# Transposing the float16 pairs of p, queries and keys: from DMA to TensorE, in an attention kernel with a gated feed-forward part

## The chip, the core and the metric

The kernel runs on one core of one Trainium2 chip. A core has TensorE (PE in the profile: matmuls out of the on-chip memory SBUF into the eight banks of PSUM; PEld is its weight load), VectorE (DVE), ScalarE (ACT), GpSimd (POOL) and SyncE (SP), which here only issues DMAs. The metric is the device time of one execution in microseconds. A time "before" and a time "after" are medians of several runs; the profile is of one execution, with its own time beside it.

## The reference

With x of 1024 rows and 512 columns, the result is x + s * g, where xn is x normalised by row:

```python
xn = _layernorm(x, axis=-1)
s = _L0_attn_ref(xn, Wq, Wk, Wv, Wo, q_norm_w, k_norm_w)
g = _silu(_L0_ffn_ref(xn, gate_w, gate_z, gate_s, up_w, up_z, up_s, down_w, down_z, down_s))
x = x + s * g
...
# attention: 32 heads in 8 groups of 4 that share keys and values, head size 128
q = _rmsnorm(q, q_norm_w)
k = _rmsnorm(k, k_norm_w)
scores = jnp.einsum('bkgqd,bksd->bkgqs', qg, k) / math.sqrt(HD)
rel = pos[None, :] - pos[:, None]
bias = jnp.where(rel > 0, NEG_INF, slopes[:, :, None, None] * rel)
attn = jax.nn.softmax(scores + bias[None], axis=-1)
out = jnp.einsum('bkgqs,bksd->bkgqd', attn, v)
return out.transpose(0, 2, 1, 3).reshape(b, s, H * HD) @ Wo.T
# feed-forward: integer weights of three matrices, dequantised by groups of 128 rows
gate = jax.nn.silu(jnp.dot(x, gate_proj))
return jnp.dot(gate * jnp.dot(x, up_proj), down_proj)
```

The attention is causal, with a bias that is linear in the distance (another slope for each head).

## The kernel before

The data is float32. Most matmuls run on pairs of float16 numbers: a value is split in a high half and what is left of it, and a product of two pairs takes three matmuls, hi*hi, hi*lo and lo*hi, into one sum. This is the helper `mm3`, whose three matmuls are lines 114, 115 and 116; so these three lines stand for many different products in the profile, told apart by the names of their tiles.

The order of the work on every engine is written out by hand, and every engine takes its instructions strictly in that order. There are three stages.

**Feed-forward (0 to about 235 us).** Layer norm, float32 transpositions of xn by TensorE (`xt_ps`, line 361, after 40 warming ones, `warm`, line 383, and a spread of the zeros, `z_ps`, line 188), gate and up products (`gu_ps`), the down product (`dn_ps`). Its result goes to `gd` in DRAM. The stage has its own PSUM pool.

**Projections (about 235 to 490 us).** Twelve projections run one after the other, each in eight tiles of 128 rows: for each pair of groups one for keys and values (`ps_kv`), then two for queries (`ps_q`, four heads each). A tile is 12 matmuls of 512 columns (`tile`, line 597). ACT copies it out (`f_q`, `f_kv`, line 607) and takes the squares (`jk`, line 609); POOL multiplies by the inverse norms; DVE makes the pair `a16` (`halves`, line 667). Scores need queries and keys with the head dimension on the partitions, so each pair has to be transposed: `transposed` (line 687) issues a transposing DMA on SP into `tr`, and `store` writes that to DRAM (`qd`, `kd`). The pairs of the last projection but one are stored as they are and transposed when they are loaded (`load_queries`, line 846); those of the last one stay in SBUF and are transposed from there (`last_queries`, line 858). With the last two projections the first eight steps of attention are interleaved (`early_tile`, line 1076).

**Attention (to the end).** A unit is one head and one block qb of 256 queries; its two steps, qt 0 and 1, are its tiles of 128 queries. The order of units goes by groups, in a group by blocks (qb 2, 3, 0, 1; the first group 3, 2, 1, 0 and the last 2, 3, 1, 0), in a block by its four heads. There are 128 units and 256 steps. Because of the causal mask, step (qb, qt) has 2*qb+qt+1 key tiles of 128. What `step` (line 1084) issues at n:

- `scores(n)` (line 903): 3 matmuls for each 512 keys into `s`, two buffers of two PSUM banks each;
- ACT: `heads_hi` (L991), when the unit whose values ended in the step before was complete;
- `biased(n-1)` on DVE (L923): scores plus bias, with the row's least; `exponentials(n-1)` on ACT (L929); `split_hi(n-3)` on ACT (L948) and `split_lo(n-4)` on DVE (L957), which make the pair of p;
- DVE: `heads_lo` (L996), then `accumulate` (L1030), which adds a finished `op` to y;
- `values(n-9)` (line 969): half of the unit's products `av` of p and values, into a bank `o`, with up to two `out_proj` in between (`op`, bank `m`, one accumulation over four heads).

`av` needs p with the keys on the partitions. So at its end `split_lo` issues a transposing DMA on SP (line 965) from `p` into `pT`, one for a step, or one for a whole unit with qb 0 (line 960), whose missing blocks are zeroed. Four `pT` buffers exist. PSUM in the last two stages: two buffers `s` of two banks each, two banks `o` and two banks `m`. SP's queue also issues every load and store.

Of the kernel before, what the change touches and what calls it, by code (L numbers as in the profile page):

```python
# [10 lines left out]
F32 = mybir.dt.float32  # L11
# [65 lines left out]
def attention_gated_by_ffn_kernel(ctx, tc, x, gu_w, gu_z, gu_s, dn_w, dn_z, dn_s, wq, wkv, wo, qnw, knw, out):  # L77
# [8 lines left out]
        return psum[0].tile([P, 2, 512], F32, tag="s", name=name)  # L86

    def ps1(tag, name):
        return psum[0].tile([P, 512], F32, tag=tag, name=name)

    def rsqrt_seed(v, y):

# [25 lines left out]

    ident = const.tile([P, P], F32, name="ident")
    make_identity(nc, ident)  # L120
    ones_bf = const.tile([P, P], BF16, name="ones_bf")
    ve.memset(ones_bf, 1.0)
    rv = const.tile([P, HKV], F32, name="rv")
# [362 lines left out]
    def finish_step():  # L486

        for f in finishing.pop(clock[0], ()):
            f()
        clock[0] += 1  # L490

    def defer(steps, f):
        finishing.setdefault(clock[0] + steps, []).append(f)
# [4 lines left out]
    class Projection:  # L498
# [98 lines left out]
        def tile(self, t):  # L597
            n, half, r = self.n, t // HT, t % HT
            if r == 0:
                self.f[half] = fq.tile([P, HT, n, HD], F32, tag="f", name=f"f_{self.name}_{half}", bufs=4)  # L600
                self.ss[half] = fq.tile([P, HT, n], F32, tag="ss", name=f"ss_{self.name}_{half}", bufs=3)
                self.jk = wp.tile([P, NH, HD], BF16, tag="jk", name=f"jk_{self.name}_{half}")
            ps = ps1("o" if t % 2 else "m", f"ps_{self.name}_{t}")
            rows = slice(t * P, (t + 1) * P)
            for j in range(KT):
                mm3(ps, (xth[:, j, rows], xtl[:, j, rows]), (self.wh[:, j, :], self.wl[:, j, :]), j == 0, j == KT - 1)
            se.copy(self.f[half][:, r], ps[:, : n * HD].rearrange("p (g d) -> p g d", g=n))
            for i in range(n):
                se.activation(
                    self.jk[:, i],  # L610
                    ps[:, i * HD : (i + 1) * HD],
                    AF.Square,
                    scale=STEEPER[i] / Q_SCALE if self.kind == "q" else 1.0,
                    accum_out=self.ss[half][:, r, i : i + 1],
                )
            if self.kind == "kv":
                if t == 0:
                    self.v16 = vp16.tile([P, 2, NT, 2, HD], F16, tag="v16", name=f"v16_{self.i}")
                v16 = self.v16[:, :, t]
                vp = ps[:, 256:512].rearrange("p (g d) -> p g d", g=2)  # L620
                se.copy(v16[:, :, 0, :], vp)
                defer(1, lambda: ve.tensor_tensor(v16[:, :, 1, :], vp, v16[:, :, 0, :], ALU.subtract))
                if t == NT - 1:
                    defer(3, self.store_values)
# [42 lines left out]
        def halves(self, t):  # L667
            f = self.f[t // HT][:, t % HT]
            n = self.n
            if self.kind == "q":  # L670
                a16 = fq.tile([P, 2, n, HD], F16, tag="a16", name=f"q16_{self.i}_{t}", bufs=5)
                hi, lo = a16[:, 0], a16[:, 1]
            else:
                a16 = fq.tile([P, 2, 2, HD], F16, tag="a16", name=f"k16_{self.i}_{t}", bufs=5)
                hi, lo = a16[:, :, 0, :], a16[:, :, 1, :]
                ve.tensor_tensor(f, f, wn.unsqueeze(1).to_broadcast([P, 2, HD]), ALU.mult)
            ve.tensor_copy(hi, f)
            ve.tensor_tensor(lo, f, hi, ALU.subtract)
            if self.k == len(projections) - 1:
                last_pairs[t] = a16  # L680
            elif self.k == len(projections) - 2:

                defer(1, lambda: sp.dma_start(qd[self.i][t], a16.rearrange("p a g d -> p (a g d)")))
            else:
                defer(1, lambda: self.transposed(t, a16))

        def transposed(self, t, a16):
            tr = fq.tile([P, 2 * self.n, P], F16, tag="tr", name=f"tr_{self.name}_{t}", bufs=5)
            sp.dma_start_transpose(tr, a16.rearrange("p a g d -> p (a g d)"))
            defer(2, lambda: self.store(t, tr))  # L690

        def store(self, t, tr):
            if self.kind == "q":
# [151 lines left out]

    def load_queries(g, qb):
        qT[g, qb] = ap1.tile([P, NQT, 2, NH, P], F16, tag="qT", name=f"qT{g}_{qb}", bufs=2)
        if g == HKV - 2:
            for i in range(NQT):
                sp.dma_start_transpose(qT[g, qb][:, i].rearrange("p a g q -> p (a g) q"), qd[g][qb * NQT + i])  # L850
            return
        sp.dma_start(
            qT[g, qb].rearrange("p t a g q -> p t (a g q)"), qd[g][qb * NQT : (qb + 1) * NQT].rearrange("t p c -> p t c")
        )
# [3 lines left out]
    def last_queries(t):  # L858
        g, qb = HKV - 1, t // NQT
        if (g, qb) not in qT:  # L860
            qT[g, qb] = ap1.tile([P, NQT, 2, NH, P], F16, tag="qT", name=f"qT{g}_{qb}", bufs=2)
        sp.dma_start_transpose(
            qT[g, qb][:, t % NQT].rearrange("p a g q -> p (a g) q"), last_pairs.pop(t).rearrange("p a g d -> p (a g d)")
        )

    def wo_squares_sums():
        ve.tensor_tensor(rvs, rv, rv, ALU.mult)
# [82 lines left out]
    def split_lo(u, qt):  # L950
        p, h16 = pf.pop((u, qt)), p16.pop((u, qt))
        nk = p.shape[1]
        if qt == 0:
            pool, tag = (wide, "wide") if u % 4 < 2 else (pt_pool, "pT")
            pT[u] = pool.tile([P, NT, 2, QB], F16, tag=tag, name=f"pT{u}", bufs=2)
        hi, lo, scale = h16[:, :, 0, :], h16[:, :, 1, :], rows16[u][3][:, qt : qt + 1]
        ve.scalar_tensor_tensor(lo, p, scale, hi, ALU.mult, ALU.subtract)  # L957
        if u in p16:
            if qt == NQT - 1:
                sp.dma_start_transpose(  # L960
                    pT[u][:, :NQT].rearrange("p t a (i q) -> p (t a i) q", i=NQT),
                    p16.pop(u).rearrange("p t a i k -> p (t a i k)"),
                )
            return
        sp.dma_start_transpose(
            pT[u][:, :nk, :, qt * P : qt * P + P].rearrange("p t a q -> p (t a) q"), h16.rearrange("p t a k -> p (t a k)")
        )

    def values(u, part, between):
# [105 lines left out]

    def early_tile(c):

        if c % 2 == 0:
            scores(*at(c // 2))
        for stage, lag in ((biased, 1), (exponentials, 2), (split_hi, 5), (split_lo, 6)):  # L1080
            if (c - lag) >= 0 and (c - lag) % 2 == 0:
                advance(stage, (c - lag) // 2)

    def step(n):
        nonlocal last_ps
        if n < nn:
            u, qt = order[n]
            g, qb, hh = units[u]
# [21 lines left out]
        if n < nn + AV_LAG + 1:  # L1110
            for due in acc_at.get(n, ()):
                accumulate(*due)
        finish_step()

        def project():
            for due in op_at.get(n, ()):
                out_proj(*due)

        if at(n - AV_LAG):
            values(*at(n - AV_LAG), project)  # L1120
        else:
            project()
# [102 lines left out]
```

## Time and profile before

| | |
|---|---|
| median of 3 runs | 1050.61 us (1048.09 to 1052.13) |
| the profiled execution | 1050.74 us, its span 1049.0 us |
| granted TensorE clock, mean | 0.991 |
| busy in the span: PE, DVE, ACT, POOL | 999.9, 877.8, 799.9, 424.3 us |
| DMA packets | 455007, of which 401474 under 512 B; 203.34 MB |
| transposing DMAs | 224 for p, 48 and 32 for queries and keys, 16 more for queries |
| median time to landing, p | 4.1 us |

A row of instructions gives the engine, the line, the tile written, the tiles read, the shape, the count, the busy time and the mean duration; then the idle time of the engine just before, with what ended it. Matmuls are pipelined: the duration of one is longer than the distance to the next, and the distance is what counts on a full PE. A stage's row has the busy time of each engine, the clock granted, the busy share of the DMA engines and GB/s.

### The profile page before, as it was taken

What the parts mean: (1) busy time and instruction counts of PE and PEld (TensorE: products, weight loads), DVE (VectorE), ACT (ScalarE), POOL (GpSimd) and SP (SyncE); (2) the same over time, 40 slices, a digit from 0 to 9 for tenths busy, and PEclk for the clock granted to TensorE, in tenths of its full rate; (3) what the DMA queues carried; (4) which work ended last, traced back from release to release, by engine and by line L of the source; (5) the groups of instructions that cost most, each with busy time, mean ns of one, the idle gap of its engine ahead of it and who ended that gap; (6) DMA issues with size and microseconds to landing.
All of it is one profiled execution on the core that took longest, in us unless ns stands there. A gap on an engine that the chain in (4) does not pass through costs nothing.

```text
span 1049.0 us, 18367 instructions
## 1 busy us (share of the span) xinstructions
PE 999.9 (95%) x5909; PEld 585.9 (56%) x5909; DVE 877.8 (84%) x1744; ACT 799.9 (76%) x2160; POOL 424.3 (40%) x408
## 2 busy tenths in 40 slices
PE   7899999999999999998999998999999999989996
PEld 4344487844444444445656566566675666655563
DVE  7988997527878969788899896998998989969985
ACT  5777645778788777878888786997887879958872
POOL 2587763123746547462226113132151131430732
PEclk9999999999999999999999999999999999999998
DMA  7123279346998989999999899999999999999995
GB/s 245 56 95 119 76 192 330 122 144 164 230 246 177 254 209 243 262 203 220 221 194 205 179 223 186 182 212 199 195 224 180 224 203 171 213 214 191 232 190 128
DMA packets 455007, 203.34 MB, mean 194 GB/s; under 512 B 401474, under 2 KB 412030, under 8 KB 454910
## 3 DMA queue, kind: packets, MB, share of 16 engines
q1 hardware_dynamic: 454910, 202.17, 87.4%
q8 instruction: 46, 0.75, 0.3%
q14 instruction: 51, 0.42, 0.1%
HBM read 76.27 MB, written 27.27 MB: 99 GB/s over the span
## 4 chain that ended last, share of the span: by engine, by line
PE 61%; DVE 11%; DMA 10%; ACT 9%; issue 7%; POOL 2%; SPq 0%; DVEq 0%; POOLq 0%; ACTq 0%
DMA pT<-p 7%; PE gu_ps L273 5%; PE ps_q L115 4%; PE ps_q L116 4%; PE ps_q L114 4%; PE s L114 4%; PE s L116 4%; PE s L115 4%; PE op L115 3%; PE op L116 3%; PE op L114 3%; PE av L114 3%; PE av L115 3%; PE av L116 3%; DVE pf L923 2%
## 5 line engine op out<-in xcount | busy, mean ns | idle before, releaser
L957 DVE SCALAR_TENSOR_TENSOR p<-pf,row,p 128x1024 f16<-128x1024 f32 (+7 forms) x256 | 222.7, 870 | 21.6 <-ACT p L948 18.6
L929 ACT ACTIVATE pf<-pf,row 128x1024 f32<-128x1024 f32 (+7 forms) x256 | 197.4, 771 | 41.6 <-DVE row L923 37.3
L923 DVE CUSTOM_DVE_ANT_0 pf<-s,trel,cs 128x1024 f32<-128x1024 f32 (+7 forms) x256 | 206.9, 808 | 24.9 <-PE s L116 24.6
L948 ACT ACTIVATE p<-pf,row 128x1024 f16<-128x1024 f32 (+7 forms) x256 | 196.5, 768 | 5.9 <-DMA pT<-p 1.0
L114 PE MATMUL av<-pT,vT 128*128 128x256 f16 (+1 forms) x640 | 168.9, 264 | 19.8 <-DMA pT<-p 19.8
L115 PE MATMUL av<-pT,vT 128*128 128x256 f16 (+1 forms) x640 | 168.9, 264 | 0.0
L116 PE MATMUL av<-pT,vT 128*128 128x256 f16 (+1 forms) x640 | 168.7, 264 | 0.0
L114 PE MATMUL s<-kT,qT 128*128 128x512 f16 (+3 forms) x384 | 125.7, 327 | 6.0 <-DVE row L923 6.0
L115 PE MATMUL s<-kT,qT 128*128 128x512 f16 (+3 forms) x384 | 125.5, 327 | 0.0
L116 PE MATMUL s<-kT,qT 128*128 128x512 f16 (+3 forms) x384 | 123.8, 327 | 0.0
L882 POOL TENSOR_SCALAR wor<-wor,rvs 128x512 f32<-128x512 f32 x32 | 52.2, 1632 | 159.1 <-DMA wor<-in_wo 105.4
L114 PEld LDWEIGHTS <-vT 128*128 128x128 f16 x640 | 63.0, 98 | 63.6 <-DMA pT<-p 13.2
L115 PE MATMUL ps_q<-wl_q,xth 128*128 128x512 f16 x256 | 97.0, 379 | 1.4 <-DVE wl_q L580 1.4
L116 PE MATMUL ps_q<-wh_q,xtl 128*128 128x512 f16 x256 | 97.0, 379 | 0.0
L114 PE MATMUL ps_q<-wh_q,xth 128*128 128x512 f16 x256 | 97.0, 379 | 0.0
L991 ACT ACTIVATE oh<-av 128x256 f16<-128x256 f32 x128 | 47.7, 373 | 62.5 <-PE av L116 61.8
L115 PE MATMUL op<-wol,oh 128*128 128x512 f16 x248 | 94.8, 382 | 0.0
L116 PE MATMUL op<-woh,ol 128*128 128x512 f16 x248 | 94.8, 382 | 0.0
L114 PE MATMUL op<-woh,oh 128*128 128x512 f16 x248 | 94.5, 381 | 0.0
L115 PEld LDWEIGHTS <-vT 128*128 128x128 f16 x640 | 63.0, 98 | 39.5 <-issue 1.2
L665 POOL TENSOR_TENSOR f_q<-f_q,inv_q 128x512 f32<-128x512 f32 x64 | 81.2, 1293 | 1.1
L889 POOL TENSOR_TENSOR wol<-wor,woh 128x512 f16<-128x512 f32 x32 | 50.8, 1588 | 65.1 <-ACT woh L888 63.3
(195 smaller groups left out, 2260.9 us busy)
## 6 DMA issues: line engine op xcount, KB each, us to landing
qd<-tr_q SPq DMA_DIRECT2D x48, 256.0 KB, 3.4
qT<-qd SPq DMA_DIRECT2D x24, 512.0 KB, 4.4
wq<-in_wq SPq DMA_DIRECT2D x32, 256.0 KB, 3.9
wo_sq<-in_wo SPq DMA_DIRECT2D x8, 1024.0 KB, 8.1
wor<-in_wo SPq DMA_DIRECT2D x32, 256.0 KB, 3.4
gui<-in_gu_w SPq DMA_DIRECT2D x13, 512.0 KB, 3.5
wkv<-in_wkv SPq DMA_DIRECT2D x16, 256.0 KB, 4.1
vd<-v SPq DMA_DIRECT2D x8, 512.0 KB, 4.7
```

Of the source, the lines that this page charges most:

```text
L114: te.matmul(ps, lhsT=lh, rhs=rh, start=first, stop=False)
L115: te.matmul(ps, lhsT=lh, rhs=rl, start=False, stop=False)
L116: te.matmul(ps, lhsT=ll, rhs=rh, start=False, stop=last)
L273: te.matmul(banks[j][:, k, :], lhsT=w[:, j, ws], rhs=x[:, j, k * 512 : k * 512 + 512], start=x is xth, stop=x is xtl)
L665: ge.tensor_tensor(f, f, ib, ALU.mult)
L882: ge.tensor_scalar(wor[g, i], wor[g, i], rvs[:, g : g + 1], None, ALU.mult)
L889: ge.tensor_tensor(wol[g, i], raw, woh[g, i], ALU.subtract)
L923: ve.tensor_tensor_reduce(p, ps, trel[g][:, S - w :], cs[:, hh : hh + 1], 3e38, ALU.add, ALU.min, least[:, c])
L929: se.activation(p, p, AF.Exp, bias=least[:, c], scale=-1.0, accum_out=total[:, c])
L948: se.activation(p16[u, qt][:, :, 0, :], pf[u, qt], AF.Copy, scale=scale[:, qt : qt + 1])
L957: ve.scalar_tensor_tensor(lo, p, scale, hi, ALU.mult, ALU.subtract)
L991: se.activation(oh, av_ps[u], AF.Copy, scale=1.0 / P_SCALE)
```

## The change

No transposing DMA is left. A new helper, `turn`, transposes up to eight 128x128 float16 tiles by TensorE into one PSUM bank `t` (two buffers), and leaves the copy from there to SBUF to be issued at the next `turn`, or at a `flush`; ACT and DVE take the copies in turn.

- For p, `split_lo` no longer issues a DMA, but puts the work on a list in pieces of at most eight tiles (`turn_later`). A piece is due two steps later. `step` takes at most one piece from the list at its beginning and one before `values`; and `values` of a unit is preceded by all pieces of it that are still on the list.
- Queries and keys are turned in `transposed`, two steps after `halves` in place of one, with the copy and the store one step later each. The last projection but one is treated like the ones before it, so its queries are loaded plainly; `last_queries` turns its pairs at once.
- The two banks for `t` come from `o` and `m`, which have one buffer each now. The projections use `o`, `m` and the `s` buffers in rotation; the last two, beside which attention begins, use `o` and `m` alone.

```diff
     def ps1(tag, name):
-        return psum[0].tile([P, 512], F32, tag=tag, name=name)
+        return psum[0].tile([P, 512], F32, tag=tag, name=name, bufs=1)
+
+    turns, ticks, leave, leaving = [], [0], [0], []
+
+    def flush():
+        while leaving:
+            leaving.pop(0)()
+
+    def turn(dst, src):
+        flush()
+        ps = psum[0].tile([P, 8, P], F16, tag="t", name=f"t{leave[0]}", bufs=2)[:, : src.shape[1]]
+        for j in range(src.shape[1]):
+            te.transpose(ps[:, j, :], src[:, j, :], ident16)
+        copy = ve.tensor_copy if leave[0] % 2 else se.copy
+        leaving.append(lambda: copy(dst, ps))
+        leave[0] += 1
+
+    def turn_later(key, dst, src):
+        n = src.shape[1]
+        for c in range(0, n, 8):
+            e = min(n, c + 8)
+            turns.append((ticks[0] + 2, key, dst[:, c:e], src[:, c:e]))
+
+    def turn_one():
+        flush()
+        if turns and turns[0][0] <= ticks[0]:
+            _, _, dst, src = turns.pop(0)
+            turn(dst, src)
+
+    def turn_all(key):
+        while any(k == key for _, k, _, _ in turns):
+            _, _, dst, src = turns.pop(0)
+            turn(dst, src)
+        flush()
...
     ident = const.tile([P, P], F32, name="ident")
     make_identity(nc, ident)
+    ident16 = const.tile([P, P], F16, name="ident16")
+    ve.tensor_copy(ident16, ident)
...
-            ps = ps1("o" if t % 2 else "m", f"ps_{self.name}_{t}")
+            name = f"ps_{self.name}_{t}"
+            if self.k < len(projections) - 2 and t % 3 == 2:
+                ps = ps2(name)[:, 0, :]
+            else:
+                ps = ps1("om"[t % 3 % 2 if self.k < len(projections) - 2 else t % 2], name)
...
             if self.k == len(projections) - 1:
                 last_pairs[t] = a16
-            elif self.k == len(projections) - 2:
-
-                defer(1, lambda: sp.dma_start(qd[self.i][t], a16.rearrange("p a g d -> p (a g d)")))
             else:
-                defer(1, lambda: self.transposed(t, a16))
+                defer(2, lambda: self.transposed(t, a16))
 
         def transposed(self, t, a16):
             tr = fq.tile([P, 2 * self.n, P], F16, tag="tr", name=f"tr_{self.name}_{t}", bufs=5)
-            sp.dma_start_transpose(tr, a16.rearrange("p a g d -> p (a g d)"))
-            defer(2, lambda: self.store(t, tr))
+            turn(tr, a16.rearrange("p a g d -> p (a g) d"))
+            defer(1, flush)
+            defer(1, lambda: self.store(t, tr))
...
         qT[g, qb] = ap1.tile([P, NQT, 2, NH, P], F16, tag="qT", name=f"qT{g}_{qb}", bufs=2)
-        if g == HKV - 2:
-            for i in range(NQT):
-                sp.dma_start_transpose(qT[g, qb][:, i].rearrange("p a g q -> p (a g) q"), qd[g][qb * NQT + i])
-            return
...
-        sp.dma_start_transpose(
-            qT[g, qb][:, t % NQT].rearrange("p a g q -> p (a g) q"), last_pairs.pop(t).rearrange("p a g d -> p (a g d)")
-        )
+        turn(qT[g, qb][:, t % NQT].rearrange("p a g q -> p (a g) q"), last_pairs.pop(t).rearrange("p a g d -> p (a g) d"))
...
             if qt == NQT - 1:
-                sp.dma_start_transpose(
+                turn_later(
+                    u,
                     pT[u][:, :NQT].rearrange("p t a (i q) -> p (t a i) q", i=NQT),
-                    p16.pop(u).rearrange("p t a i k -> p (t a i k)"),
+                    p16.pop(u).rearrange("p t a i k -> p (t a i) k"),
                 )
             return
-        sp.dma_start_transpose(
-            pT[u][:, :nk, :, qt * P : qt * P + P].rearrange("p t a q -> p (t a) q"), h16.rearrange("p t a k -> p (t a k)")
+        turn_later(
+            u,
+            pT[u][:, :nk, :, qt * P : qt * P + P].rearrange("p t a q -> p (t a) q"),
+            h16.rearrange("p t a k -> p (t a) k"),
         )
...
     def early_tile(c):
+        ticks[0] += c % 2
+        turn_one()
         if c % 2 == 0:
             scores(*at(c // 2))
...
     def step(n):
         nonlocal last_ps
+        ticks[0] += 1
+        turn_one()
         if n < nn:
...
         finish_step()
+        turn_one()
...
         if at(n - AV_LAG):
+            turn_all(at(n - AV_LAG)[0])
             values(*at(n - AV_LAG), project)
```

## The prediction

> **What bounds the kernel now.** I read the page's busy rows first, then the same rows by stage, then who makes TensorE (PE) wait, then single instructions, since a busy PE need not be a PE at its peak.
>
> The page, its head and its first rows:
>
> ```profile
> span 1049.0 us, 18367 instructions
> PE 999.9 (95%) x5909; PEld 585.9 (56%) x5909; DVE 877.8 (84%) x1744; ACT 799.9 (76%) x2160; POOL 424.3 (40%) x408
> ```
>
> The stages (feed-forward to 235, projections to 490, attention to the end; PE, PEld, DVE, ACT, POOL busy, then clock and DMA share):
>
> ```profile
> 0.00:235.00 235.00, 219.30 (x997) 128.99 (x998) 180.89 (x238) 157.55 (x252) 120.73 (x71) 0.99 0.48 153
> 235.00:490.00 255.00, 251.97 (x1236) 119.23 (x1235) 209.43 (x435) 205.33 (x899) 134.52 (x190) 1.00 0.98 222
> 490.00:1049.00 559.00, 528.60 (x3681) 337.70 (x3678) 487.51 (x1071) 437.05 (x1011) 169.03 (x149) 0.99 1.00 198
> ```
>
> PE is idle 3 us in the projections and 30 us in attention; DMA is full in both. PE's idle time, by what ended it (sum, times, longest):
>
> ```profile
> PE av L114 <- DMA pT<-p: 19.8, 14, 2.9
> PE s L114 <- DVE row L923: 6.0, 8, 2.1
> ```
>
> So the transposing DMAs, though full, cost PE only 19.8 us. The chain of waits says more ("DMA pT<-p 7%"), but a chain counts time in which PE had other work; 1049.0 - 999.9 = 49.1 us bounds what PE can gain from any wait.
>
> Is the busy PE at peak? Single instructions (start, duration):
>
> ```profile
> 639.79 0.27 PE L114 MATMUL av<-pT,vT 128*128 128x256 f16 x1
> 639.90 0.27 PE L115 MATMUL av<-pT,vT 128*128 128x256 f16 x1
> 640.12 0.22 PE L114 MATMUL s<-kT,qT 128*128 128x128 f16 x1
> 640.17 0.22 PE L115 MATMUL s<-kT,qT 128*128 128x128 f16 x1
> 640.23 0.22 PE L116 MATMUL s<-kT,qT 128*128 128x128 f16 x1
> 641.27 0.38 PE L114 MATMUL op<-woh,oh 128*128 128x512 f16 x1
> 641.48 0.38 PE L115 MATMUL op<-wol,oh 128*128 128x512 f16 x1
> ```
>
> Starts are 0.215 us apart for 512 columns, 0.11 for 256, 0.055 for 128, each with its own weight load: the cost follows the columns, nothing lies between. PE is truly full, and work added to it in these two stages is added to the time.
>
> **The change part by part.**
>
> *PE, added.* For p, per head and block of 256 queries, the two query tiles have 2qb+1 and 2qb+2 key tiles, each as two halves: 14, 22 and 30 transpositions for qb 1, 2, 3, and 8 for qb 0 (zero blocks included). That is 74 per head, times 32 heads: 2368. Queries: seven projections x 8 tiles x 8 = 448, the last one 64. Keys: 4 x 8 x 4 = 128. Together 3008, in 448 turns of up to eight. The nearest row is the 128-column f16 matmul with its own load, 0.0556 us: 3008 x 0.0556 = 167 us, of it (448 + 128) x 0.0556 = 32 in the projections and 135 in attention.
>
> Against that stand the transpositions the kernel has, in float32: 16 of xt_ps from 25.06 to 27.49, 0.144 us each, but there the weight load alone takes 0.141 (0.098 for f16). And the Trainium skill, TensorE: Matmul & The Clock Gate, Part 4: PE-mode transpose, speaks against the change: about 275 ns per transposition inside a kernel, and transpositions don't count as activity that keeps the clock up. As a cadence 275 ns would be 827 us. The trace disagrees on both:
>
> ```profile
> 1.36 6.68 PE L383 MATMUL warm<-ident 128*128 128x128 f32 x40 [1.36 <-POOL ident masks.py:199]
> 7.97 0.60 PE L188 MATMUL z_ps<-z,pick 14*128 14x512 f16 x2
> ```
>
> 40 transpositions take 0.17 us each from cold, and of the two matmuls behind them the second starts 0.60 - 0.38 = 0.22 us after the first, full clock: 275 ns is a latency, and transpositions do warm the clock. I take 0.0556. The lower end is the columns (0.053); the upper is one exposed weight load, 0.098: 295 us. Nothing allows a gain here.
>
> *Copies out of PSUM, added.* ACT takes even turns, DVE odd ones; turns per unit make ACT get most full ones: per head 42 tiles in 5.5 turns on ACT, 32 in 5.5 on DVE. ACT: f_q 0.585 us for 512 and f_kv 0.370 for 256 columns, so 0.16 + 0.00083 per column, less 0.09 that neighbours overlap: 32 x (42 x 128 x 0.00083 + 5.5 x 0.07) = 155 us. DVE has float32 rows from PSUM (L923: 0.740 at 512, 1.277 at 1024: 0.2 + 0.00104 per column, 0.065 overlapped): 32 x (32 x 128 x 0.00104 + 5.5 x 0.14) = 161 us. The Trainium skill, VectorE: DVE Perf Modes, Why PSUM operands drop a tier, allows two elements a cycle for 16-bit data out of PSUM and one for float32: 93 us. No row here reads 16 bits from PSUM. The attention sums become PE 528.6 + 135 = 664, ACT 437 + 155 = 592, DVE 487 + 93 = 580 or + 161 = 648. PE stays largest either way, so the copies cost nothing by themselves; I take the rule's end, since the row's data type is the wrong one. By block the cover holds too: at qb 3, per head, PE 5.5 to 6.8, ACT 4.5 to 6.3, DVE 5.2 to 6.0 (6.5 by the row); at qb 2 and 1 the row's end would put DVE up to 0.25 above PE, some 10 us in all. In the projections the copies are 34 us on ACT and 25 on DVE, beside PE 252 + 32 = 284: hidden.
>
> *DMA, removed.* 320 transposing transfers leave SP's queue: L965 alone held it 1.2 to 3.7 us apiece; queries of the last but one group are stored transposed, so those loads become plain. Loads queued behind them on SP come earlier. No PE wait is on such a load, so that is worth nothing; POOL's 105 us for wor are cover-less idling of an engine at 40%. What counts is the 19.8 us, and the slow stretch that follows a long one: after the 2.8 us at 646.8 matmuls run at half pace for 3.4 us, losing 1.7; three waits of that size make 5. I credit 25; bounds 0 and 30. Late next is the copy on ACT or DVE, issued at the following turn, but av comes two steps after its last turn, and a step is over 2 us.
>
> *PSUM, moved.* The two banks of t come from o and m, one each now. First, av of the next unit must wait for L991 and L996 of the last, 0.375 + 0.417 and two hand-offs, say 0.9 us; PE has between them its scores (0.17 to 1.3) and its turns (up to 0.44 each). In blocks qb 0 and 1 about 0.3 shows, 64 x 0.3 = 19 us; elsewhere it is hidden if ACT and DVE come in time. Second, out_proj's next tile waits for accumulate (L1030, 0.743), queued on DVE behind L923, L957 and L996 of that step: 64 tiles, perhaps 0.15 each, 10. Queued behind a waiting PE are the following scores, for which DVE and ACT then wait, so a delay goes round. Third, the last two projections run on two banks in place of four: ACT's 1.5 us per tile are hidden by the next tile's 2.6 unless exponentials lie between; 16 tiles, 0.4 each, 6. Sum 35; below nothing it cannot be (fewer buffers), above 100 (0.4 us in each of 256 steps).
>
> Sum against the profiled execution: 1050.7 (span 1049.0 and 1.7 around it; the median of the runs, 1050.6, is the same) + 167 - 25 + 35 = 1228.
>
> **The rivals.**
>
> *A bank wait becomes the bound.* The turns have two banks; in heavy steps two turns run, so PE's first turn of a step waits for a copy that stands last on ACT's or DVE's queue of the step before. For it: the three engines would be within 13% of each other, none with slack for a lock step. Against: copies have a step's length. At 0.25 us more in each of 256 steps it is 1228 + 64 = 1292.
>
> *The transposition is not hidden behind its weight load.* For it: the float32 rows above. Against: f16 128-column matmuls follow each other at 0.055 with loads of 0.098 in flight. At 0.098: 1228 + 128 = 1356.
>
> *Faster: the DMA was the real bound.* For it: the chain has DMA at 10%, 105 us, DMA is full, and PE's clock dips after such waits. If these were all given back and the new work lay in holes of PE, time would be near 1049 - 25 = 1025. It decides at 49.1 us / 3008 = 0.016 us: a transposition has to cost less than that. Its 128 columns take 0.053, so I see no way.
>
> **How the numbers follow.** A measurement here tells about 0.5%, 5 us, from no change. PE-bound as summed: 0.62, 1190 to 1260. Bank waits or DVE at one element a cycle on top: 0.24, 1260 to 1330. Weight loads exposed: 0.06, above 1330. Cheaper than summed, with no bank waits, yet slower: 0.05, under 1190. Faster 0.02, no change 0.01. Leaving out the top and the bottom gives 1185 to 1315.
>
> **What would show it.** Right: some 3000 new f16 matmuls into t, starts 0.055 to 0.06 apart; PE busy near 1150; pT<-p gone from the waits and the chain; DMA share of both later stages well under half; DVE's copies from t near 0.74 us for 1024 columns, ACT's near 1.0; the projection stage 32 us longer; new PE waits on DVE and ACT of 20 to 60 us. Wrong: matmuls into t 0.1 us apart; DVE over 95% in attention; PE waiting at each turn for a copy; or a span under 1100, which would mean that PE was not full.

## The result, and the profile after

The changed kernel takes 1233.16 us (median of 3 runs, 1233.11 to 1233.69), against 1050.61 us before: slower, ratio 1.1743 (95% interval 1.1706 to 1.178). The prediction was 1228 us. The profiled execution is one of these, 1233.16 us with a span of 1231.4 us, and a mean granted clock of 0.999 where it was 0.991.

The page of the changed kernel, its head, the busy rows and the DMA totals:

```profile
span 1231.4 us, 23758 instructions
PE 1169.6 (95%) x8917; PEld 752.3 (61%) x8917; DVE 990.5 (80%) x1969; ACT 985.7 (80%) x2384; POOL 401.6 (33%) x408
...
DMA packets 60849, 107.16 MB, mean 87 GB/s; under 512 B 6274, under 2 KB 16830, under 8 KB 60734
```

There are 3008 matmuls more and 394,000 DMA packets fewer; those under 512 bytes fell from 401,474 to 6274. PE's share is the same 95%: its busy time rose by 169.7 us and its idle time from 49.1 to 61.8, which is the 182.4 us of the span. ACT gained 186 us of work, more than PE, and DVE 113.

The changed kernel by stage (feed-forward, projections, attention; columns: length, busy time of PE, PEld, DVE, ACT, POOL, then granted clock, DMA share, GB/s). The last projection now ends 35 us later, so the second border has moved from 490 to 525:

```profile
0.00:235.00 235.00, 219.62 (x1005) 129.15 (x1006) 181.90 (x242) 157.86 (x253) 121.43 (x72) 1.00 0.48 155
235.00:525.00 290.00, 283.04 (x1847) 151.58 (x1845) 237.72 (x476) 239.51 (x940) 122.27 (x186) 1.00 0.39 125
525.00:1231.00 706.00, 666.92 (x6071) 471.58 (x6068) 570.88 (x1253) 588.36 (x1193) 157.93 (x150) 1.00 0.14 49
```

The first stage is untouched. The projections grew by 35 us and attention by 147. DMA, full in both before, is at 0.39 and 0.14, and the time did not follow it down. In attention ACT is at 588 of 706 and DVE at 571: the distance of PE to the next engine, ACT, is 79 us; before it was 41, to DVE. The copies keep both engines close behind PE.

Who makes PE wait in the changed kernel (sum, times, longest):

```profile
PE av L149 <- DVE ol L1032: 16.1, 32, 1.4
PE op L149 <- DVE y L1066: 11.1, 14, 1.1
PE t L103 <- DVE tr_q L105: 3.9, 5, 0.8
PE t L103 <- ACT pT L105: 3.5, 10, 0.6
...
PE op L149 <- DVE y L1064: 1.6, 2, 1.1
...
PE t L103 <- DVE pT L105: 1.3, 3, 0.8
```

The 19.8 us for `pT<-p` are gone, and so are the 6.0 for the row of `biased`. In their place PE waits 16.1 us for the one bank `o` (av must wait until `heads_lo`, L1032 now, has read it), 13.9 for the one bank `m` (op behind the three lines of `accumulate`; the third, 1.2 us, is not shown) and 9.9 for a bank of `t`: 39.9 us in all.

Single instructions of the changed kernel in the projections (start, duration):

```profile
271.27 0.38 PE L151 MATMUL ps_q<-wh_q,xtl 128*128 128x512 f16 x1
...
271.49 0.61 PE L103 MATMUL t<-ident,q 128*128 128x128 f16 x8
...
271.93 0.38 PE L149 MATMUL ps_q<-wh_q,xth 128*128 128x512 f16 x1
```

A turn (one call of `turn`, here of eight transpositions) starts 0.22 us after the matmul ahead of it and holds PE for 0.44 us until the next one starts: 0.055 us for each transposition. Within it, the last starts 0.61 - 0.219 = 0.39 us after the first, 0.056 apart.

The copies out of `t` in attention, by shape (count, then busy time and mean ns of one, then idle time ahead of them and its cause):

```profile
L105 ACT COPY pT<-t 128x1024 f16<-128x1024 f16 x140 | 139.3, 995 | 3.3 <-PE t L103 3.3
L105 DVE COPY pT<-t 128x1024 f16<-128x1024 f16 x84 | 57.5, 684 | 21.1 <-PE t L103 20.9
L105 DVE COPY pT<-t 128x256 f16<-128x256 f16 x31 | 9.0, 291 | 13.1 <-PE t L103 12.8
```

ACT's 177 copies of p take 167.5 us and DVE's 175 take 95.7; ACT has most of the full turns. ACT hardly ever waits for its copy's data, 3.3 us in 140 copies: it comes to them late.

### The profile page after: what moved, and what is told of

It reads as the page before. It is cut to its first block, busy times and chain, and to the rows that moved or that the text cites. A ratio compares the mean times of both kernels' runs of the same rounds, so it can differ in the third digit from the quotient of the medians.

```text
span 1231.4 us, 23758 instructions
## 1 busy us (share of the span) xinstructions
PE 1169.6 (95%) x8917; PEld 752.3 (61%) x8917; DVE 990.5 (80%) x1969; ACT 985.7 (80%) x2384; POOL 401.6 (33%) x408
## 4 chain that ended last, share of the span: by engine, by line
PE 74%; DVE 12%; ACT 10%; issue 3%; DMA 1%; POOL 0%; SPq 0%; DVEq 0%; POOLq 0%; ACTq 0%
PE t L103 10%; PE gu_ps L310 5%; PE av L149 5%; PE ps_q L149 4%; PE ps_q L151 4%; PE ps_q L150 4%; PE av L151 4%; PE av L150 4%; PE s L151 4%; PE s L149 4%; PE s L150 4%; PE op L149 4%; PE op L150 3%; PE op L151 3%; ACT p L981 2%
## 5 line engine op out<-in xcount | busy, mean ns | idle before, releaser
L990 DVE SCALAR_TENSOR_TENSOR p<-pf,row,p 128x1024 f16<-128x1024 f32 (+7 forms) x256 | 213.5, 834 | 8.9 <-ACT p L981 7.4
L103 PE MATMUL t<-ident,p 128*128 128x128 f16 x2368 | 189.6, 219 | 9.3 <-DVE tr_q L105 3.9
L149 PE MATMUL av<-pT,vT 128*128 128x256 f16 (+1 forms) x640 | 167.5, 262 | 16.4 <-DVE ol L1032 16.1
L103 PEld LDWEIGHTS <-p 128*128 128x128 f16 x2368 | 155.2, 98 | 27.1 <-issue 12.1
L105 ACT COPY pT<-t 128x1024 f16<-128x1024 f16 (+2 forms) x177 | 167.5, 946 | 3.3 <-PE t L103 3.3
L150 PE MATMUL av<-pT,vT 128*128 128x256 f16 (+1 forms) x640 | 167.5, 262 | 0.0
L105 DVE COPY pT<-t 128x1024 f16<-128x1024 f16 (+3 forms) x175 | 95.7, 547 | 60.6 <-PE t L103 60.0
L922 POOL TENSOR_TENSOR wol<-wor,woh 128x512 f16<-128x512 f32 x32 | 45.0, 1407 | 281.9 <-ACT woh L921 281.9
L149 PE MATMUL op<-woh,oh 128*128 128x512 f16 x248 | 93.9, 379 | 13.9 <-DVE y L1066 11.1
L150 PEld LDWEIGHTS <-vT 128*128 128x128 f16 x640 | 62.5, 98 | 51.7 <-issue 20.2
```

Of the source, the lines that this page charges most:

```text
L103: te.transpose(ps[:, j, :], src[:, j, :], ident16)
L105: leaving.append(lambda: copy(dst, ps))
L149: te.matmul(ps, lhsT=lh, rhs=rh, start=first, stop=False)
L150: te.matmul(ps, lhsT=lh, rhs=rl, start=False, stop=False)
L922: ge.tensor_tensor(wol[g, i], raw, woh[g, i], ALU.subtract)
```

## The experiments

The theory was the prediction's sum: PE is full, 3008 transpositions of 0.056 us are added, the banks given to `t` cost some waits, the copies nothing. The rival was that ACT and DVE, with the copies on their queues, have become a limit of their own. Each difference below is against runs of the kernel before that were taken beside it (their medians are 1047.94, 1049.94, 1047.69 and 1050.98 us in four groups).

**The banks alone (e1_banks).** The kernel before, with its DMAs, but one bank each of `o` and `m`, and the rotation of the changed kernel in the projections:

```diff
-        return psum[0].tile([P, 512], F32, tag=tag, name=name)
+        return psum[0].tile([P, 512], F32, tag=tag, name=name, bufs=1)
...
-            ps = ps1("o" if t % 2 else "m", f"ps_{self.name}_{t}")
+            name = f"ps_{self.name}_{t}"
+            if self.k < len(projections) - 2 and t % 3 == 2:
+                ps = ps2(name)[:, 0, :]
+            else:
+                ps = ps1("om"[t % 3 % 2 if self.k < len(projections) - 2 else t % 2], name)
```

> The kernel before, with its DMA transposes, but with one buffer each of o and m, and the tiles of the projections spread over o, m and s as in the changed kernel; the two banks that come free stay unused. The theory (columns on a full PE are the bulk, the lost banks a small part): only the bank waits come, 25 to 50 us, so 1075 to 1100 us, with PE waiting on L996 and L1030's lines (ol, y) for 20 us or more each way. The rival (lock step by the missing banks is what costs): 1130 us or more. A third possibility, that the banks cost nothing: within 5 us of 1050.

Measured: 1102.48 us, +54.5, ratio 1.052 (1.05 to 1.0541), just above what was expected; the waits for the bank `m`, behind `accumulate` (14.6 us with the rows not shown), stayed below the 20 that were forecast. PE's waits in it:

```profile
PE av L114 <- DVE ol L1000: 49.5, 71, 2.6
PE op L114 <- DVE y L1034: 11.3, 14, 2.0
```

So with nothing else changed, the banks cost more than the 35 us of the prediction, and the `ol` wait is three times that of the changed kernel. There the turns are work that PE can do while it would otherwise wait; e7_columns_only below tests that.

**Which bank (e11_single_m).** The same with `o` back at two banks:

```diff
-        return psum[0].tile([P, 512], F32, tag=tag, name=name, bufs=1)
+        return psum[0].tile([P, 512], F32, tag=tag, name=name, bufs=2 if tag == "o" else 1)
```

> The kernel before with one bank m and two banks o (one bank unused). e1_banks, with both single, took 1102.5 us, with PE waits of 50 us for ol and 15 for y. If the two losses add as these waits say: about 12 to 18 us over the kernel before, 1060 to 1066. If the ring through o only shows because of m: 25 us or more.

Measured: 1072.29 us, +24.6, ratio 1.0229 (1.0192 to 1.0267). That is near the rival's mark and not at the theory's. Taken in this order, `m` is worth 25 of the 54.5 us and `o` the other 30; no run has a single `o` alone.

**Queries and keys on PE, p by DMA (e3_proj_only).** The changed kernel with the two transposing DMAs of `split_lo` put back (one of the two places is shown):

```diff
-        turn_later(
-            u,
-            pT[u][:, :nk, :, qt * P : qt * P + P].rearrange("p t a q -> p (t a) q"),
-            h16.rearrange("p t a k -> p (t a) k"),
-        )
+        sp.dma_start_transpose(
+            pT[u][:, :nk, :, qt * P : qt * P + P].rearrange("p t a q -> p (t a) q"), h16.rearrange("p t a k -> p (t a k)")
+        )
```

> The changed kernel with p transposed by DMA as before: TensorE turns queries and keys only (640 transpositions, 576 of them in the projections), with the changed bank layout. The theory: e1_banks plus 32 us in the projection stage plus 3.6 us for the last queries, so 30 to 38 us above e1_banks. The rival (relief of the DMA queue pays for some of it): less than 20 us above e1_banks.

Measured: 1134.68 us, +86.7, ratio 1.0831 (1.0813 to 1.085), 32.2 above e1_banks and within the 30 to 38 expected. The difference holds 640 transpositions, 576 in the projections and the last queries' 64, which are 35.7 us at 0.0558: in the projections PE has hardly a hole, and a turn is paid nearly in full. PE's waits in attention are nearly those of e1_banks:

```profile
PE av L149 <- DVE ol L1029: 44.4, 68, 2.3
PE op L149 <- DVE y L1063: 11.1, 14, 2.0
```

**The columns of p without their copies (e7_columns_only).** e3_proj_only, and beside its DMAs PE also transposes p, into a `t` that nothing reads:

```diff
         sp.dma_start_transpose(
             pT[u][:, :nk, :, qt * P : qt * P + P].rearrange("p t a q -> p (t a) q"), h16.rearrange("p t a k -> p (t a k)")
         )
+        turn_later(u, None, h16.rearrange("p t a k -> p (t a) k"))
...
+        if dst is None:
+            return
         copy = ve.tensor_copy if leave[0] % 2 else se.copy
```

> e3_proj_only (p by DMA) with the transpositions of p by TensorE added into the banks t, which nothing reads: the columns without the copies. If the columns on a full PE are the cost: 1134.7 + 132 less the bank waits that they cover (PE waits 57 us on ol and y in e3_proj_only, of which some 25 to 40 go): 1225 to 1245 us. If they lie in waits that the copies and the bank o make anyway: less than 60 us above e3_proj_only, under 1195.

Measured: 1198.2 us, +148.3, ratio 1.1404 (1.136 to 1.1448): between the two expectations, neither met. p's 2368 transpositions added 148.3 - 86.7 = 61.6 us, and not 132. PE's waits, and the attention stage of this kernel (columns as above):

```profile
PE av L151 <- DVE ol L1034: 4.5, 16, 1.3
PE op L151 <- DVE y L1068: 3.8, 13, 0.3
```

```profile
522.00:1196.00 674.00, 658.13 (x6033) 469.00 (x6031) 507.43 (x1079) 446.84 (x1018) 166.35 (x149) 1.00 0.82 162
```

PE is at 658 of 674. Some 50 us of new columns went where PE had been waiting for a bank (55.5 us in the two rows of e3, 8.3 here). The busy rows of e3_proj_only and of this kernel say the same:

```profile
PE 1048.3 (93%) x6549; PEld 620.6 (55%) x6549; DVE 922.8 (82%) x1793; ACT 837.6 (74%) x2208; POOL 413.4 (37%) x408
PE 1164.4 (97%) x8917; PEld 752.8 (63%) x8917; DVE 928.6 (78%) x1793; ACT 842.3 (70%) x2208; POOL 411.3 (34%) x408
```

With spans of 1131.9 and 1196.1 us, PE's idle time fell from 83.6 to 31.7 us and its busy time rose by 116.1. That is 16 less than 2368 times 0.0558; what makes up these 16 is not shown. This is the prediction's sum with the copies at nothing (but with p's DMAs still there), and it is 1198, not 1228: most of the 35 us of bank waits that were added to the sum are covered. From here to the changed kernel p's DMAs go and its copies come, and that costs another 182.6 - 148.3 = 34.3 us. PE waits for no DMA of p in e7_columns_only, so their going can have given back little.

**The copies of p without their columns (e4_p_copies_only).** The changed kernel without p's transpositions: the copies read p in SBUF and write it, not transposed, where they did. All else is as changed, with the banks `t` held for queries and keys:

```diff
-        ps = psum[0].tile([P, 8, P], F16, tag="t", name=f"t{leave[0]}", bufs=2)[:, : src.shape[1]]
-        for j in range(src.shape[1]):
+        if times:
+            ps = psum[0].tile([P, 8, P], F16, tag="t", name=f"t{leave[0]}", bufs=2)[:, : src.shape[1]]
+        for j in range(src.shape[1] * times):
             te.transpose(ps[:, j, :], src[:, j, :], ident16)
...
-        leaving.append(lambda: copy(dst, ps))
+        leaving.append(lambda: copy(dst, ps if times else src))
...
             _, _, dst, src = turns.pop(0)
-            turn(dst, src)
+            turn(dst, src, 0)
```

> The changed kernel without the transpositions of p: the copies go from the pair of p straight to pT, untransposed, so that attention weights meet the wrong values (this part of the computation is changed). Turns, lists and their order stay; banks t are used by queries and keys alone. The theory: PE loses 132 us of work and becomes lighter than ACT (about 590 us of a stage of 600), so the time falls by 70 to 110 us, to 1125 to 1165, with ACT then the fullest engine. The rival (copies or bank waits set the step): it falls by less than 40, to 1195 or more.

Measured: 1200.31 us, +152.4, ratio 1.1452 (1.1435 to 1.1469). The theory missed widely and the rival held: with 132 us of PE's work gone, only some 30 us came back. PE's waits and the attention stage (from 522, as in e7_columns_only):

```profile
PE av L150 <- DVE ol L1033: 88.9, 97, 3.3
PE op L150 <- DVE y L1067: 16.2, 19, 1.8
```

```profile
522.00:1198.00 676.00, 559.51 (x3779) 346.65 (x3776) 557.81 (x1248) 584.87 (x1188) 156.12 (x150) 0.98 0.15 51
```

PE is busy for 560 of 676 us and waits over 100 for the two banks, twice as long as in e3_proj_only: `heads_hi` and `heads_lo`, which free `o`, stand in queues that are longer by a copy. ACT's copies took 1030 ns for 1024 columns out of SBUF (995 out of PSUM) and DVE's 590 (684), so the copies' load on the queues is about the same as in the changed kernel.

**Are these the banks, then? (e8_copies_two_o, e12_copies_all_banks.)** The first is e4_p_copies_only with two banks of `o` and one of `t`:

```diff
-        return psum[0].tile([P, 512], F32, tag=tag, name=name, bufs=1)
+        return psum[0].tile([P, 512], F32, tag=tag, name=name, bufs=2 if tag == "o" else 1)
...
-            ps = psum[0].tile([P, 8, P], F16, tag="t", name=f"t{leave[0]}", bufs=2)[:, : src.shape[1]]
+            ps = psum[0].tile([P, 8, P], F16, tag="t", name=f"t{leave[0]}", bufs=1)[:, : src.shape[1]]
```

> e4_p_copies_only (copies of p without transposing it, which changes this part of the computation) with two buffers of o and one of t. e4_p_copies_only took 1200 us with no engine full and 89 us of PE waits for ol. If the single bank o makes that second limit: these waits go to under 15 us and the time falls to 1100 to 1135. If it is the work of the copies on ACT (616 us of 708 busy) and DVE: it stays above 1165.

Measured: 1194.64 us, +144.7, ratio 1.1365 (1.1316 to 1.1413), again above the mark of the rival. The wait moved to the other bank; and with a granted clock of 0.962, against 0.986 in e4_p_copies_only, PE's matmuls took longer, so the pair of banks `o` may be worth more than the time says:

```profile
PE op L150 <- DVE y L1067: 65.5, 41, 4.1
PE op L150 <- DVE y L1065: 11.7, 7, 2.8
```

So another run was made with both pairs of banks back. It has no bank `t`: queries and keys are turned in banks `m`.

```diff
-        return psum[0].tile([P, 512], F32, tag=tag, name=name, bufs=1)
+        return psum[0].tile([P, 512], F32, tag=tag, name=name, bufs=2)
...
-            ps = psum[0].tile([P, 8, P], F16, tag="t", name=f"t{leave[0]}", bufs=2)[:, : src.shape[1]]
+            ps = ps1("m", f"t{leave[0]}").bitcast(F16).rearrange("p (c q) -> p c q", q=P)[:, : src.shape[1]]
```

> e4_p_copies_only (p copied untransposed, which changes this part of the computation) with two banks each of o and m, as before the change; the few turns of queries and keys use the banks m. The last of the runs on what holds the copies without the columns near 1200 us, where one bank o more (1194.6) and less work on ACT (1201.9) did nothing. If it is the pair of single banks, in which every late instruction of DVE stops PE: it falls to 1100 to 1140, and PE waits for ol and y under 25 us. If the copies by themselves, in their place in the queues of ACT and DVE, hold it: above 1165, with the waits only moved to other instructions.

Measured: 1157.5 us, +106.5, ratio 1.1012 (1.0966 to 1.1058), between the two expectations. The attention stage (from 522) and PE's longest wait:

```profile
522.00:1155.00 633.00, 551.84 (x3775) 347.96 (x3772) 558.35 (x1252) 584.76 (x1193) 155.30 (x150) 0.99 0.15 54
```

```profile
PE s L150 <- DVE row L957: 64.0, 63, 2.3
```

The waits for `o` and `m` have left PE's list, and PE now waits for `biased` on DVE to free the scores' banks. So of e4_p_copies_only's time the banks are 152.4 - 106.5 = 46 us. Of the other 106.5, 32 are the turns of queries and keys, if they cost here what they cost in e3_proj_only, and some 75 come with p's copies: ACT is at 92% and DVE at 88% of the stage, in queues whose order is fixed, and PE waits 64 us for what stands on them.

**Doubling the columns (e2_p_twice).** The changed kernel, each transposition of p issued twice into the same tile:

```diff
         for j in range(src.shape[1]):
-            te.transpose(ps[:, j, :], src[:, j, :], ident16)
+            for _ in range(times):
+                te.transpose(ps[:, j, :], src[:, j, :], ident16)
...
             _, _, dst, src = turns.pop(0)
-            turn(dst, src)
+            turn(dst, src, 2)
```

> The changed kernel with every transposition of p issued twice in a row, the second over the first: 2368 more TensorE instructions, copies and banks the same. The theory (PE is full, 0.0557 us for each): 2368 x 0.0557 = 132 us more, less some bank waits that the longer steps hide: 1350 to 1365 us, transpositions still 0.056 us apart. The rival (copies or bank waits set the step, and transpositions lie in PE's waits): less than 80 us more, under 1315.

Measured: 1335.08 us, +287.1, ratio 1.2742 (1.2723 to 1.2761): 104.5 us more than the changed kernel's 182.6, neither the theory's 117 or more nor below the rival's mark. A doubled turn (start, duration) and PE's waits:

```profile
900.48 1.06 PE L104 MATMUL t<-ident,p 128*128 128x128 f16 x16
```

```profile
PE av L150 <- DVE ol L1033: 5.7, 8, 1.2
...
PE op L150 <- DVE y L1067: 2.9, 7, 0.7
```

The distance is still (1.06 - 0.219) / 15 = 0.056 us, so 2368 more are 132 us of PE's time. The bank waits fell from 30.0 to 10.5 (the rows shown and two of `accumulate`, 1.9), the waits for a bank of `t` from 9.9 to 5.9, and PE's idle time in all from 61.8 to 38.7: once more columns first fill waits. Doubling an operation that has waits beside it measures less than its price.

**Who copies (e5_all_act, e6_all_dve, e9_swapped).** One line of the changed kernel, three ways: all copies on ACT, all on DVE, and the two engines exchanged, so that DVE takes the even turns, which have more of the full ones.

```diff
-        copy = ve.tensor_copy if leave[0] % 2 else se.copy
+        copy = se.copy                                           # e5_all_act
+        copy = ve.tensor_copy                                    # e6_all_dve
+        copy = se.copy if leave[0] % 2 else ve.tensor_copy       # e9_swapped
```

> The changed kernel with all copies from t on ACT. ACT would have some 740 us of work in attention against PE's 667: if the copies are hidden only by the slack of the engine that has them, 70 to 110 us more, 1305 to 1345. If PE's columns alone set the step: under 30 us more.

Measured: 1288.55 us, +238.6, ratio 1.2268 (1.222 to 1.2317): 56 above the changed kernel, less than the first expectation, more than the rival's bound. PE's largest group of waits is now for a copy, 44.1 us, and ACT is busy for 710 of the 764 us from 525 to the end.

```profile
PE t L103 <- ACT pT L105: 44.1, 56, 2.4
```

> The changed kernel with all copies from t on DVE: DVE about 690 us in attention, ACT 421, PE 667. If the amount of copying counts, DVE is a little over PE: 1235 to 1265. If what counts is that a copy of 1 us stands in ACT's queue ahead of L1027, so that the bank o comes free late: a little faster, 1205 to 1225.

Measured: 1253.57 us, +203.6, ratio 1.193 (1.1875 to 1.1985): 21 above the changed kernel, as expected if it is the amount of work on DVE that counts. The wait for `o`, 16.1 us in the changed kernel, grows with DVE's longer queue:

```profile
PE av L149 <- DVE ol L1032: 37.7, 61, 1.4
```

> The changed kernel with the two engines of the copies exchanged: DVE takes the even turns (42 tiles for each head in place of 32), ACT the odd ones. ACT loses some 34 us of work in attention, DVE gains about 21. If ACT is a second limit beside PE's columns, as the run without columns says: 8 to 20 us faster than the changed kernel, 1213 to 1225. If PE's columns alone set the step: within 4 us of 1233.

Measured: 1219.7 us (1219.17 to 1221.43), +172.0, ratio 1.164 (1.1608 to 1.1671), as expected if ACT limits beside PE. Its attention:

```profile
525.00:1218.00 693.00, 664.16 (x6061) 471.23 (x6058) 591.98 (x1252) 556.97 (x1191) 163.13 (x150) 1.00 0.15 50
```

Against the changed kernel 31 us went from ACT and 21 came to DVE; PE's work is the same, and the stage is 10 to 14 us shorter. This is the best version found, and still far slower than the kernel before.

**ACT's copies to POOL (e10_copies_pool).** e4_p_copies_only, with POOL in the place of ACT for p:

```diff
-        copy = ve.tensor_copy if leave[0] % 2 else se.copy
+        copy = ve.tensor_copy if leave[0] % 2 else se.copy if times else ge.tensor_copy
```

> e4_p_copies_only (p copied untransposed, which changes this part of the computation) with ACT's half of these copies on POOL, which was 23% busy in attention. If the work of the copies on ACT is what holds that kernel at 1200 us, although PE has no transposition of p: it falls to 1135 to 1160, near e3_proj_only. If the order of the lists and the single banks hold it: above 1180. POOL's copies may slow DVE where they overlap, which would leave it between the two.

Measured: 1201.92 us, +154.2, ratio 1.1468 (1.1432 to 1.1504). Read by the expectation, ACT was not the cause. But the experiment moved a second thing, as its attention shows (from 522):

```profile
522.00:1198.00 676.00, 562.11 (x3772) 339.17 (x3772) 614.64 (x1246) 446.03 (x1016) 358.45 (x316) 0.98 0.14 51
```

ACT fell by 139 us against e4_p_copies_only, and DVE rose by 57 with the same instructions: the mean of `split_lo` went from 847 to 922 ns, and that of DVE's copies from 459 to 734. So it tells nothing on ACT. The rows stand in the last section.

## Why the prediction was right, and where it was not

The time was right, and most steps with it, but in part by luck: two terms were wrong by about the same amount, in opposite directions. The terms, in its own order:

| term | predicted | measured |
|---|---|---|
| columns of 3008 transpositions | +167 | PE busy +169.7; starts 0.056 apart |
| of it in the projections | 32 | 32.2 (e3_proj_only less e1_banks, with the 64 of the last queries) |
| waits for the DMAs of p | -25 with slow stretches | 19.8 gone; clock 0.991 to 0.999 |
| wait for `o` | 19 | 16.1 |
| wait for `m` | 10 | 13.9 |
| last two projections on two banks | 6 | 0: no wait of their matmuls for a bank |
| wait of turns for a bank of `t` | named as a rival | 9.9, of it 5.1 behind copies of `tr` |
| copies out of PSUM | 0 | 34.3, between e7_columns_only and the changed kernel |

*The cadence.* It is that of the plain 128-column f16 matmul, and with twice as many in a row it stays. The rival with an exposed weight load (0.098) is out. (The lower end of 0.053 is 0.054 by the prediction's own 0.215 us for 512 columns.) Its support was misread: the 0.144 us of `xt_ps` is a mean with pauses in it. The warming transpositions, also float32, show the pace, early and late in their row:

```profile
2.69 2.12 PE L383 MATMUL warm<-ident 128*128 128x128 f32 x9
6.13 1.36 PE L383 MATMUL warm<-ident 128*128 128x128 f32 x11
```

The first nine start (2.12 - 0.42) / 8 = 0.21 us apart and the later eleven (1.36 - 0.27) / 10 = 0.11 (0.42 and 0.27 are the durations of one), less than the 0.141 that a weight load of `xt_ps` takes: the loads overlap there too. Nothing but transpositions had run on PE until then, so its pace rose under them alone, as the prediction held.

*The faster rival.* DMA was full and the chain ran through it, but with the DMAs gone the time rose, and only the 19.8 us of PE's waits for them can be seen to have come back. No run takes the DMAs away alone. The chain had counted time in which PE had other work.

*The copies' durations.* DVE took 684 ns for 1024 columns. The sum's end, two elements a cycle (0.74), held; one element a cycle would have been 0.2 + 1.07 = 1.27 us. From 256 columns (291 ns) to 1024 a column costs 0.51 ns, half of the 1.04 in the float32 rows. This is the rule of the Trainium skill, VectorE: DVE Perf Modes, Why PSUM operands drop a tier, for 16-bit data out of PSUM, and the trace agrees: DVE's rows in float32 were the wrong ones to take. ACT, with 995 ns, was as its rows had said.

*The lock step at the turns.* This rival asked for a wait at each turn; PE waits 9.9 us for `t` in the whole kernel.

*The step that failed.* "PE stays largest either way, so the copies cost nothing by themselves." The first half is true, and the second does not follow from it. The chain of differences, in us over the kernel before, shows it:

| | over before | step |
|---|---|---|
| one bank each of `o` and `m` (e1_banks) | 54.5 | 54.5 |
| and queries and keys on PE (e3_proj_only) | 86.7 | 32.2 |
| and p's columns, its DMAs kept (e7_columns_only) | 148.3 | 61.6 |
| and p's copies, its DMAs gone (the changed kernel) | 182.6 | 34.3 |

Without the copies, PE's new columns cover the bank waits almost wholly (9.8 us left in e7_columns_only, all rows), so the 35 us entered for banks would not have shown. With the copies, PE's idle time goes from 31.7 to 61.8 us and its waits for the two banks from 9.8 back to 30.0. The waits that the prediction listed under "PSUM, moved" are there, at nearly its size, but it takes both to make them: a single bank, and a longer queue in front of the instruction that frees it. So the banks should have stood at some 10, the copies at some 34. Without the copies the sum would have been 30 us too high, as e7_columns_only shows: 1228 against 1198.

One such place in the changed kernel (start, duration, engine; in brackets the idle time before and what ended it):

```profile
800.62 0.22 PE L151 MATMUL av<-pT,vT 128*128 128x128 f16 x1
...
800.94 0.99 ACT L105 COPY pT<-t 128x1024 f16<-128x1024 f16 x1
...
801.98 0.61 PE L103 MATMUL t<-ident,p 128*128 128x128 f16 x8 [0.37 <-ACT pT L105]
802.35 0.38 ACT L1027 ACTIVATE oh<-av 128x256 f16<-128x256 f32 x1
...
802.76 0.42 DVE L1032 SCALAR_TENSOR_TENSOR ol<-av,oh 128x256 f16<-128x256 f32 x1 [0.41 <-ACT oh L1027]
...
803.24 0.27 PE L149 MATMUL av<-pT,vT 128*128 128x256 f16 x1 [0.66 <-DVE ol L1032]
```

`av` is complete at 800.84, but `heads_hi` comes on ACT only at 802.35, behind `split_hi`, a copy of 0.99 us and a cast of `woh` of 0.62, all queued ahead of it; DVE then waits for ACT, and PE, which has done its scores and two turns by then, for DVE.

The wider finding is that there are two limits of nearly one height. PE's columns without p's copies take 1198 us; p's copies without its columns take 1200 us; together they take 1233. Both of the first two contain e3_proj_only's 86.7 us for banks, queries and keys. Above that the columns add 61.6 us, the copies 65.7 (with p's DMAs gone), and both together 95.9, not 127.3: about half of each is hidden by the other. That ACT was the tighter of the two copiers is suggested by e9_swapped (10 to 14 us for 31 us less of ACT's work and 21 more of DVE's), though the exchange also changes which copy stands where in the queues; the prediction's attention sums for ACT and DVE, 592 and 580, were right to 2% (588 and 571, from 525 on), but were only held against PE's sum, as if an engine at 83% had no say.

What stays open: how the second limit divides between busy time on ACT, on DVE, and the fixed order. No run issues the same copies at another place, behind `heads_hi` for example. e12_copies_all_banks puts 46 us of e4_p_copies_only to the banks and leaves some 75 to the copies, with a turn's cost taken from another kernel; e10_copies_pool, which should have separated ACT from DVE, slowed DVE.

## What to carry to other kernels

When PE is full and hardly waits for a DMA, however full that is, moving the DMA's work to PE costs PE's time for the new columns. Take the gain from PE's waits for the DMA, and not from the DMA's share or the chain. Then look at the queues, not only at the largest sum: here copies on in-order engines that were busy for 80% of the time delayed whatever frees PSUM behind them, and taking banks from double buffers makes PE feel each such delay. And a cost that fills waits looks small: remove and add each part alone, since two limits of one height hide one another.

## What the runs showed of the hardware that was not expected

POOL copying float16 from SBUF to SBUF slows DVE's work beside it. The expectation of e10_copies_pool named this as possible; its size is new. `split_lo` takes 922 ns in place of the 847 of e4_p_copies_only, DVE's copies 734 in place of 459, and DVE's busy time in the stage rises from 558 to 615 us. Within e10_copies_pool, DVE's copies of 1024 columns that meet no POOL instruction take 416 ns on average (35 of 84), those that meet a POOL copy 1071 (28). The POOL copies themselves (mean 1122 ns over all sizes, 196.6 us) are slower than ACT's from the same place (982 ns in e4_p_copies_only). First three rows of e10_copies_pool, then two of e4_p_copies_only:

```profile
L106 POOL COPY pT<-p 128x1024 f16<-128x1024 f16 (+2 forms) x177 | 196.6, 1122 | 240.9 <-DVE p L991 197.7 <-PE s L152 31.0 <-DVE pT L106 12.2
L106 DVE COPY pT<-p 128x1024 f16<-128x1024 f16 (+3 forms) x175 | 128.2, 734 | 0.0
L991 DVE SCALAR_TENSOR_TENSOR p<-pf,row,p 128x1024 f16<-128x1024 f32 (+7 forms) x256 | 236.2, 922 | 5.6 <-ACT p L982 3.3
...
L991 DVE SCALAR_TENSOR_TENSOR p<-pf,row,p 128x1024 f16<-128x1024 f32 (+7 forms) x256 | 216.8, 847 | 22.6 <-ACT p L982 20.0
L106 DVE COPY pT<-p 128x1024 f16<-128x1024 f16 (+3 forms) x175 | 80.0, 459 | 0.0
```

In e8_copies_two_o a wait of PE of 4 us, below, was followed by matmuls at half pace (the `op` matmuls of 512 columns start 0.43 us apart, where 0.215 is usual), as in the kernel before after its wait of 2.8 us; its attention had a mean granted clock of 0.95, the lowest of these runs. In the changed kernel, whose longest wait for a bank is 1.4 us, the clock is 0.999.

```profile
712.63 0.59 PE L150 MATMUL op<-woh,oh 128*128 128x512 f16 x1 [4.05 <-DVE y L1067]
713.01 0.63 PE L151 MATMUL op<-wol,oh 128*128 128x512 f16 x1
713.44 0.63 PE L152 MATMUL op<-woh,ol 128*128 128x512 f16 x1
```
